# A second pair of heads in seven block products instead of eight, at the start of a fused two-layer block

## The chip, the cores and the metric

The kernel runs on one core of a Trainium2 chip. A core has TensorE (matmuls; PE in the profile), VectorE (DVE), ScalarE (ACT) and GpSimd (POOL), and SyncE (SP), whose queue issues most of the DMAs. The metric is device time in microseconds (us) of one launch, the median over several runs.

## The reference

Eight sequences of 128 tokens by 512 channels go through four residual steps, each of the form x = x + tanh(gate) * f(layernorm(x)): a cross attention with 32 heads and position biases, a dense layer with 4-bit weights, a cross attention with one head, and a dense layer with a router and low-rank experts. The change touches the first attention:

```python
h_q = (x @ w_q.T).reshape(b, lq, H, DH)            # H = 32 heads of DH = 128
h_k = (key_value_states @ w_k.T).reshape(b, lk, H, DH)
score = jnp.einsum('bqhd,bkhd->bhqk', h_q, h_k) + position_bias[None]
```

and the router's map from 15 outputs to 8 experts:

```python
mapped = expert_map[topk_i]
onehot = (mapped[..., None] == jnp.arange(E)).astype(x.dtype)
```

## The kernel before

**Exactness.** Every float32 operand of a large matmul is split into a high part (a rounded copy, made on ScalarE) and a low part (the rest, by a subtraction on VectorE or GpSimd); `split` (L168) does both. A product is then three matmuls, high by high, high by low, low by high (`product`, L172).

**Keys and queries.** Heads are worked in 16 pairs. For one pair and all tokens the product is a 2 by 2 matrix of blocks of weights (two heads by two halves of the 512 channels) times a 2 by 2 matrix of blocks of the context (two halves of the channels by two halves of the tokens: B11, B12, B21, B22). Done plainly that is eight block products; `project_plainly` (L568) makes it with 48 matmuls of 128x512 (lines 591 to 593) and four copies out (L597). `seven` (L214) makes it with seven block products, P1, P5, P6, P2, P7, P4, P3, of six matmuls each (lines 178, 179, 182), which need sums and differences of blocks on both sides:

- of the context, T1 to T4, made once in `context_operands` (L460): differences on VectorE (L488), high parts on ScalarE (L471), low parts one half on GpSimd and one half on VectorE (L474);
- of the weights, for each pair: `pair_sums` (L296) makes three sums on VectorE (L303 to L305), and `pair_parts` (L308) splits the seven parts (L169 and L170) and makes the fourth sum (L315). With `BY_POOL`, the low parts of P1, P2 and P4 are GpSimd's.

The products of `seven` share three PSUM banks: P1, P6, P7 and P4 add up in the same bank c1, and ScalarE copies it out in between (L246, L253, L262, L268); VectorE adds the others (L257, L263, L272).

**The order.** `keys_and_queries` (L953) walks over the pairs. The first two (`PLAIN = 2`) are made plainly, since T1 to T4 are not there yet; in the same stretch the context's differences and pair 2's parts are made. From then on the products of a pair stand among the last ones of the pair before (L974), the parts of the next pair are cast between them, and the normalised rows of x for the queries are made (`query_operands`, L492: statistics, scaling L451 and L454, transposes L505).

TensorE's order is the order written (`in_order`). On the other engines a scheduler sets the order when the program is built; `behind(name)` asks that an instruction be placed behind a marked one on the same engine, and is no wait. Buffers come from rings by tag: the raw weights have 7 buffers (`raw`), so a load can wait for the casts of an earlier pair.

**The experts' map.** `ffn1_weights` (L1383), which belongs to the last layer, loads the map `em_i`, casts it to float (L1397) and compares it with the expert numbers (L1401, L1404). The load and the cast have no inputs from elsewhere, so the scheduler places them early, among the first pairs.

Of the kernel before, what the change touches and what calls it, by code (L numbers as in the profile page):

```python
# [66 lines left out]
def kernel(  # L67
# [37 lines left out]
    nc = tc.nc  # L105
# [9 lines left out]
    def slot(shape, tag, name, dtype=F32):  # L115
        return sb.tile(shape, dtype, tag=tag, name=name, bufs=TAGS[tag])

    def page(shape, name, dtype=F32R):


        return slot(shape, "page", name, dtype)

    def wide_row(tag, name, dtype=F32):
        return slot([P, D], tag, name, dtype)
# [4 lines left out]
    def wide(t):  # L129

        return t.bitcast(F32)


    marks = {}
# [4 lines left out]
    @contextmanager  # L139
    def behind(*names):  # L140
        with ExitStack() as stack:
            for name in names:
                stack.enter_context(tc.issue_after(marks[name]))
            yield
# [23 lines left out]
    def split(high, low, src, low_engine=None):  # L168
        mark("high", nc.scalar.copy(high, src))  # L169
        mark("low", (low_engine or nc.vector).tensor_tensor(low, src, wide(high), ALU.subtract))  # L170
# [105 lines left out]
    def run(steps):  # L276
        for _ in steps:
            pass
# [4 lines left out]
    def load(key, src, shape=(P, D)):  # L283
        t = slot(list(shape), "raw", f"raw_{key}")
        mark("load", nc.sync.dma_start(out=t, in_=src))
        raws[key] = t

    def load_pair(kind, p):
        if p < NP:
            w = {"wk": wk, "wq": wq}[kind]  # L290
            for h in (2 * p, 2 * p + 1):
                load(f"{kind}_{h}", w[:, h])
# [15 lines left out]
    def pair_parts(kind, p, sums, parts, by_pool=()):  # L308

        for which in LEFT:  # L310
            t = parts[which] = slot([P, 2, N], "v", f"{kind}{which}_{p}", F32R)
            with behind("copy"):
                split(t[:, 0], t[:, 1], sums[which], nc.gpsimd if which in by_pool else nc.vector)
            if which == "P2":
                nc.vector.tensor_tensor(sums["P3"], sums["P2"], sums["P6"], ALU.subtract)  # L315
            yield
# [143 lines left out]
    def context_operands():  # L460

        ops = right_pages("cx")
        ops["B12"] = page([P, 2, HK, HALF * P], "cxB12")
        blocks = {
            n: [cx_raw.pop((half, 2 * inner + i)) for i in range(HK)]
            for n, half, inner in (("B11", 0, 0), ("B12", 1, 0), ("B21", 0, 1), ("B22", 1, 1))
        }

        def put(n, i, src, engine=nc.vector):
            o = ops[n]  # L470
            nc.scalar.copy(o[:, 0, i, :], src)  # L471
            mark(
                "low",
                engine.tensor_tensor(o[:, 1, i, :], src, wide(o[:, 0, i, :]), ALU.subtract),  # L474
            )

        for n, pair in blocks.items():
            for i, t in enumerate(pair):
                put(n, i, t)
        marks["lows"] = marks["low"]  # L480
        yield ops
        b11, b12, b21, b22 = blocks.values()
        for n, dst, one, two in (
            ("T1", b11, b12, b11), ("T2", b11, b22, b11), ("T3", b12, b22, b12), ("T4", b21, b21, b11)
        ):
            for i in range(HK):
                with behind("lows"):
                    nc.vector.tensor_tensor(dst[i], one[i], two[i], ALU.subtract)  # L488
                    put(n, i, dst[i], (nc.gpsimd, nc.vector)[i])
        yield ops  # L490
# [424 lines left out]
    BY_POOL = ("P1", "P2", "P4")  # L915
    BEFORE = NP - 2
    order = [("keys", p) for p in range(BEFORE)] + [("queries", p) for p in range(NP)]
    order += [("keys", p) for p in range(BEFORE, NP)]
    def whole_pair(p):

        both, rows = [], []
        for h in range(2 * p, 2 * p + 2):
            both.append([wide_row("v", f"wk_{n}{h}", F32R) for n in "hl"])
            t = raws.pop(f"wk_{h}")
            rows.append(t if p else t.rearrange("p dc n -> p (dc n)"))
        step = D if p else N
        for at in range(0, D, step):
            for (high, low), t in zip(both, rows):
                cols = slice(at, at + step)
                split(high[:, cols], low[:, cols], t[:, cols])  # L930
        return both

    PLAIN = 2

    def later():

        return behind(*(n for n in ("copy", "add") if n in marks))

    left = whole_pair(0)
    making = context_operands()  # L940
# [3 lines left out]
    sums, before = None, iter(())  # L944

    def sums_of(n):
        if n < len(order):
            k, q = order[n]
            return pair_sums("w" + k[0], q)
# [3 lines left out]
    def keys_and_queries():  # L953
        nonlocal left, sums, before
        for n, (kind, p) in enumerate(order[:-1]):
            if n < PLAIN:
                if n + 2 < len(order):
                    load_pair("w" + order[n + 2][0][0], order[n + 2][1])
                if n + 1 == PLAIN:
                    following = {}  # L960
                    run(pair_parts("wk", n + 1, sums_of(n + 1), following))
                    sums = sums_of(n + 2)
                project_plainly(kind, p, left, of_context)
                left = following if n + 1 == PLAIN else whole_pair(p + 1)
                if n == 0:
                    next(making)
                continue
            following = {}
            k, q = order[n + 1]
            casts = pair_parts("w" + k[0], q, sums, following, BY_POOL if n < BEFORE else ())  # L970
            now = project(kind, p, left, of_context if kind == "keys" else rows[-1])
            left = following

            for i, which in enumerate((now, now, before, now, before, now, now)):  # L974
                next(which, None)
                next(casts, None)
                if n == BEFORE // 2 and i == 3:

                    with later():
                        rows.append(next(of_rows))  # L980
                if i == 0:
                    if n + 2 < len(order):
                        load_pair("w" + order[n + 2][0][0], order[n + 2][1])
                    else:
                        load_quad(0)
            before = now
            with behind("add"):
                sums = sums_of(n + 2)
            if n == 3:
                with later():  # L990
                    prep_mask()
            if n < BEFORE:
                with later():
                    rows.append(next(of_rows))
            if 14 <= n < 14 + NB:
                with later():
                    residual(n - 14)
            if n >= BEFORE - 3:
                for _ in range(2 - n % 2):
                    next(extra, None)  # L1000
        parts = quad_parts(0)
        for _ in range(2):
            next(parts)
        for u in range(FIRST):
            fetch(u)
        run(before)
        run(extra)
        run(parts)

    with in_order(*ORD):  # L1010
        keys_and_queries()
# [371 lines left out]
    def ffn1_weights():  # L1383
        for dc in range(NDC):
            t = page([P, 2, 2, NS], f"bw{dc}")
            nc.sync.dma_start(out=wide(t).rearrange("p a h n -> p a (h n)"), in_=bw_kept[:, dc])
            for half in range(2):
                bw[dc, half] = [t[:, part, half] for part in range(2)]
        t = page([P, 2, D], "lora")
        nc.sync.dma_start(out=wide(t), in_=lora_kept)  # L1390
        lora.extend(t[:, part] for part in range(2))
        nc.sync.dma_start(out=rb, in_=router_b.partition_broadcast(P))

        em_i = keep([P, NR], "em_i", I32)
        nc.sync.dma_start(out=em_i, in_=expert_map.partition_broadcast(P))
        em_f = keep([P, NR], "em_f")
        nc.vector.tensor_copy(em_f, em_i)  # L1397
        e_i = slot([P, NE, NR], "moved", "e_i", I32)
        nc.gpsimd.iota(e_i, pattern=[[1, NE], [0, NR]], base=0, channel_multiplier=0)
        nc.vector.tensor_copy(twice, e_i)  # L1400
        nc.vector.tensor_tensor(  # L1401
            twice, twice, em_f.unsqueeze(1).to_broadcast([P, NE, NR]), ALU.is_equal
        )
        nc.vector.tensor_scalar_mul(twice, twice, 2.0)  # L1404
        yield
# [123 lines left out]
```

## Time and profile before

| | us |
|---|---|
| median of 3 runs | 908.09 (907.79 to 909.52) |
| span of the profiled execution | 907.1 |
| TensorE busy | 900.8 (99%) |
| VectorE busy | 673.1 (74%) |
| ScalarE busy | 503.0 (55%) |
| GpSimd busy | 460.3 (51%) |
| first pair's matmuls begin | 5.21 |
| second pair's matmuls, plain | 17.46 to 28.34 |
| third pair's first matmul | 28.34 |

Times in the profile count from the start of the span. A line of a timeline gives the start, the time from first start to last end, the engine, the line of the code, the operation, output and inputs, shapes, and how many instructions were merged; in brackets stands the idle time of that engine before it and what ended it. Matmuls overlap, so their durations are longer than their distance; the distance is read from the starts.

### The profile page before, as it was taken

What the parts mean: (1) busy time and instruction counts of PE and PEld (TensorE: products, weight loads), DVE (VectorE), ACT (ScalarE), POOL (GpSimd) and SP (SyncE); (2) the same over time, 40 slices, a digit from 0 to 9 for tenths busy, and PEclk for the clock granted to TensorE, in tenths of its full rate; (3) what the DMA queues carried; (4) which work ended last, traced back from release to release, by engine and by line L of the source; (5) the groups of instructions that cost most, each with busy time, mean ns of one, the idle gap of its engine ahead of it and who ended that gap; (6) DMA issues with size and microseconds to landing.
All of it is one profiled execution on the core that took longest, in us unless ns stands there. A gap on an engine that the chain in (4) does not pass through costs nothing.

```text
span 907.1 us, 16427 instructions
## 1 busy us (share of the span) xinstructions
PE 900.8 (99%) x5381; PEld 799.2 (88%) x5381; DVE 673.1 (74%) x1353; ACT 503.0 (55%) x1426; POOL 460.3 (51%) x513
## 2 busy tenths in 40 slices
PE   9999999999999999999999999999999999999998
PEld 7888888888888899999999999999999998888897
DVE  7888878789889866777677667666686877565587
ACT  6666555667555545545536445453454544588862
POOL 2355534114322436756747657583866844265441
PEclk9999999999999999999999999999999999999999
DMA  7755477889875956667574765766767566814001
GB/s 256 255 162 163 152 205 232 294 280 285 275 238 204 298 196 186 182 193 221 163 238 151 203 215 153 222 176 201 215 165 208 180 178 177 306 47 143 1 24 71
DMA packets 125223, 174.99 MB, mean 193 GB/s; under 512 B 17105, under 2 KB 54737, under 8 KB 124113
## 3 DMA queue, kind: packets, MB, share of 16 engines
q1 hardware_dynamic: 124992, 173.68, 61.5%
q8 instruction: 42, 0.69, 0.3%
q14 instruction: 45, 0.36, 0.1%
q10 hardware_dynamic: 144, 0.26, 0.1%
HBM read 109.86 MB, written 64.03 MB: 192 GB/s over the span
## 4 chain that ended last, share of the span: by engine, by line
PE 93%; DVE 3%; DMA 2%; ACT 1%; issue 0%; POOL 0%; SPq 0%; DVEq 0%; ACTq 0%; POOLq 0%
PE c_v L178 7%; PE c_v L179 6%; PE c_v L182 6%; PE pso L182 6%; PE pso L178 6%; PE pso L179 6%; PE sc L692 6%; PE av L756 6%; PE c_q L178 6%; PE c_q L179 6%; PE c_q L182 6%; PE c_k L178 4%; PE c_k L179 4%; PE c_k L182 4%; PE tph L1127 1%; DMA cxraw<-in_cxT_dram 1%
## 5 line engine op out<-in xcount | busy, mean ns | idle before, releaser
L709 ACT ACTIVATE s<-s,nm 128x128 f32<-128x128 f32 x256 | 99.8, 392 | 78.8 <-DVE nm L699 54.8
L777 DVE SCALAR_TENSOR_TENSOR x<-pso,tg,x 128x512 f32<-128x512 f32 x128 | 93.4, 741 | 52.2 <-PE pso L182 51.3
L717 POOL TENSOR_TENSOR s<-s,rs 128x512 f32<-128x512 f32 x64 | 66.7, 1042 | 111.1 <-DVE rs L715 63.2
L178 PE MATMUL pso<-wo_h,a 128*128 128x512 f32 x256 | 101.9, 411 | 0.0
L179 PE MATMUL pso<-wo_l,a 128*128 128x512 f32 x256 | 101.5, 397 | 0.0
L182 PE MATMUL pso<-wo_h,a 128*128 128x512 f32 x256 | 101.0, 395 | 0.1
L178 PE MATMUL c_v<-wvP,cxT 128*128 128x256 f32 x288 | 84.8, 294 | 0.2 <-ACT v L253 0.2
L182 PE MATMUL c_v<-wvP,cxT 128*128 128x256 f32 x288 | 81.4, 283 | 0.0
L179 PE MATMUL c_v<-wvP,cxT 128*128 128x256 f32 x288 | 81.4, 283 | 0.0
L757 ACT CAST a<-av 128x512 fp32r<-128x512 f32 x64 | 37.4, 584 | 74.4 <-PE av L756 74.0
L679 POOL TENSOR_TENSOR s<-mneg,bias 128x512 f32<-128x512 bf16 x64 | 75.9, 1186 | 0.1
L756 PE MATMUL av<-pT,v 128*128 128x128 f32 x512 | 71.2, 274 | 0.0
L756 PEld LDWEIGHTS av<-pT,v 128*128 128x128 f32 x512 | 67.1, 191 | 2.8
L692 PE MATMUL sc<-k,q 128*128 128x128 f32 x464 | 65.8, 274 | 0.0
L692 PEld LDWEIGHTS sc<-k,q 128*128 128x128 f32 x464 | 61.9, 191 | 3.2
L178 PE MATMUL c_v<-wvP,cxB 128*128 128x256 f32 x216 | 62.1, 289 | 0.0
L758 DVE TENSOR_TENSOR a<-av,a 128x512 fp32r<-128x512 f32 x64 | 43.4, 679 | 24.9 <-ACT a L757 24.5
L179 PE MATMUL c_v<-wvP,cxB 128*128 128x256 f32 x216 | 61.2, 283 | 0.0
L182 PE MATMUL c_v<-wvP,cxB 128*128 128x256 f32 x216 | 61.1, 283 | 0.0
L170 POOL TENSOR_TENSOR wo_l<-raw_wo,wo_h 128x512 fp32r<-128x512 f32 x32 | 41.4, 1293 | 33.8 <-ACT wo_h L169 33.8
L182 PEld LDWEIGHTS pso<-wo_h,a 128*128 128x128 f32 x256 | 48.2, 188 | 10.8 <-DVE a L758 1.3
L695 DVE TENSOR_TENSOR s<-sc,s 128x512 f32<-128x512 f32 x64 | 43.7, 683 | 17.1 <-PE sc L692 12.4
(277 smaller groups left out, 2808.4 us busy)
## 6 DMA issues: line engine op xcount, KB each, us to landing
keys<-keys SPq DMA_DIRECT2D x64, 256.0 KB, 3.5
queries<-queries SPq DMA_DIRECT2D x64, 256.0 KB, 3.5
through<-s SPq DMA_DIRECT2D x64, 256.0 KB, 2.6
moved<-through SPq DMA_DIRECT2D x256, 64.0 KB, 3.0
q<-queries SPq DMA_DIRECT2D x58, 256.0 KB, 3.8
k<-keys SPq DMA_DIRECT2D x58, 256.0 KB, 4.3
raw_wq<-in_wq_dram SPq DMA_DIRECT2D x32, 256.0 KB, 3.9
raw_wv<-in_wv_dram SPq DMA_DIRECT2D x32, 256.0 KB, 4.9
```

Of the source, the lines that this page charges most:

```text
L170: mark("low", (low_engine or nc.vector).tensor_tensor(low, src, wide(high), ALU.subtract))
L178: nc.tensor.matmul(out, lhsT=lh, rhs=rh, start=first, stop=False, **more)
L179: nc.tensor.matmul(out, lhsT=lh, rhs=rl, start=False, stop=False, **more)
L182: nc.tensor.matmul(out, lhsT=ll, rhs=rh, start=False, stop=last, **more),
L679: nc.gpsimd.tensor_tensor(s, mneg[:, half], bias.unsqueeze(2).to_broadcast([P, NQ, HALF, Q32]), ALU.add)
L692: nc.tensor.matmul(ps[:, j, :], lhsT=q[:, cols], rhs=k[:, cols], start=True, stop=True)
L695: nc.vector.tensor_tensor(s, by_block(ps), s, ALU.add)
L709: e = nc.scalar.activation(one, one, AF.Exp, bias=nm[:, j : j + 1], accum_out=sm[:, j : j + 1])
L717: mark(f"norm{u}", nc.gpsimd.tensor_tensor(s, s, factors, ALU.mult))
L756: nc.tensor.matmul(av[:, b, :], lhsT=v[:, cols], rhs=pT[:, b, :], start=True, stop=True)
L758: mark("al", nc.vector.tensor_tensor(al, av, wide(ah), ALU.subtract))
L777: "x", nc.vector.scalar_tensor_tensor(xs[b], ps, factor, xs[b], ALU.mult, ALU.add, **out)
```

## The change

`PLAIN` becomes 1: only the first pair is made plainly. Behind it the rest of the context's operands (T1 to T4) is made, then the parts of the second pair (called pair 1 in the code, as counting starts at 0), with GpSimd's share as for the later pairs; the second pair goes through `seven`. The load of pair 2's weights stays, and pair 3's loads are issued in the step of the second pair. In `pair_parts` the mark "copy" is used only where it exists. The first rows of x are still made from the same step on (`PLAIN < n`). The cast of the experts' map is placed behind the latest low part of the attention's output ("al"), near the end.

```diff
@@ pair_parts
-            with behind("copy"):
+            with behind(*("copy",) * ("copy" in marks)):
                 split(t[:, 0], t[:, 1], sums[which], nc.gpsimd if which in by_pool else nc.vector)
@@
-    PLAIN = 2
+    PLAIN = 1
@@ keys_and_queries
             if n < PLAIN:
-                if n + 2 < len(order):
-                    load_pair("w" + order[n + 2][0][0], order[n + 2][1])
-                if n + 1 == PLAIN:
-                    following = {}
-                    run(pair_parts("wk", n + 1, sums_of(n + 1), following))
-                    sums = sums_of(n + 2)
+                load_pair("wk", 2)
                 project_plainly(kind, p, left, of_context)
-                left = following if n + 1 == PLAIN else whole_pair(p + 1)
-                if n == 0:
-                    next(making)
+                next(making)
+                left = {}
+                run(pair_parts("wk", 1, sums_of(1), left, BY_POOL))
+                sums = sums_of(2)
                 continue
@@
-            if n < BEFORE:
+            if PLAIN < n < BEFORE:
                 with later():
                     rows.append(next(of_rows))
@@ ffn1_weights
         em_f = keep([P, NR], "em_f")
-        nc.vector.tensor_copy(em_f, em_i)
+        with behind("al"):
+            nc.vector.tensor_copy(em_f, em_i)
```

## Prediction

> **What bounds the kernel now.** I read the page's busy line and the shares of the chain first, then who TensorE waited for, then each engine's timeline around the changed place, 12 to 29 us. The page:
>
> ```profile
> PE 900.8 (99%) x5381; PEld 799.2 (88%) x5381; DVE 673.1 (74%) x1353; ACT 503.0 (55%) x1426; POOL 460.3 (51%) x513
> ...
> PE 93%; DVE 3%; DMA 2%; ACT 1%; issue 0%; POOL 0%; SPq 0%; DVEq 0%; ACTq 0%; POOLq 0%
> ```
>
> All the waits of TensorE in the whole span (longest us last):
>
> ```profile
> PE idle L412 <- POOL ident masks.py:199: 1.4, 1, 1.4
> PE tpx L505 <- DVE xq L454: 0.5, 1, 0.5
> PE c_k L591 <- ACT cxB L471: 0.5, 1, 0.5
> PE c_v L178 <- ACT v L253: 0.2, 1, 0.2
> ```
>
> TensorE is the path. Behind 5.2 us it waits 0.5 + 0.2 us until the last stage, so a matmul removed is time gained, and, just as much, a hole made early is found again at the end: nothing later is there to swallow it. TensorE's timeline, at the start, where the second pair begins, and where it ends:
>
> ```profile
> 5.80 0.63 PE L592 MATMUL c_k<-cxB,wk_l 128*128 128x512 f32 x1
> 6.22 0.63 PE L593 MATMUL c_k<-cxB,wk_h 128*128 128x512 f32 x1
> 6.65 0.52 PE L591 MATMUL c_k<-cxB,wk_h 128*128 128x512 f32 x1
> ...
> 17.46 0.39 PE L591 MATMUL c_k<-cxB,wk_h 128*128 128x512 f32 x1
> ...
> 28.34 0.39 PE L178 MATMUL c_k<-cxB,wkP 128*128 128x512 f32 x1
> ```
>
> From 17.46 to 28.34 stand the 48 matmuls of the second pair in the plain way, 10.88 us or 0.2267 us each, without a hole. In that same time the other engines make the differences of the context (T1 to T4), which the plain way does not need. VectorE, GpSimd and ScalarE:
>
> ```profile
> 14.01 0.68 DVE L170 TENSOR_TENSOR wk_l<-raw_wk,wk_h 128x512 fp32r<-128x512 f32 x1
> 14.62 1.78 DVE L488 TENSOR_TENSOR cxraw<-cxraw,cxraw 128x512 f32<-128x512 f32 x1
> 18.13 2.48 DVE L488 TENSOR_TENSOR cxraw<-cxraw,cxraw 128x512 f32<-128x512 f32 x4
> 20.54 5.19 DVE L474 TENSOR_TENSOR cxT<-cxraw,cxT 128x512 fp32r<-128x512 f32 x3
> ```
> ```profile
> 14.28 1.57 POOL L474 TENSOR_TENSOR cxT<-cxraw,cxT 128x512 fp32r<-128x512 f32 x1 [12.95 <-ACT cxT L471]
> 19.53 5.64 POOL L474 TENSOR_TENSOR cxT<-cxraw,cxT 128x512 fp32r<-128x512 f32 x3 [3.69 <-ACT cxT L471]
> ```
> ```profile
> 18.84 1.67 ACT L471 CAST cxT<-cxraw 128x512 fp32r<-128x512 f32 x3 [3.11 <-DVE cxraw L488]
> 21.88 1.15 ACT L471 CAST cxT<-cxraw 128x512 fp32r<-128x512 f32 x2
> ```
>
> A VectorE subtraction of 128x512 costs 0.62 us alone (2.48 for four). Beside GpSimd's it costs 1.73 (5.19 for three): the two engines take turns, and a turn of both is 0.61 + 1.13. So the differences are ready only at 25.2 (GpSimd) and 25.7 (VectorE). Today nobody waits: TensorE first reads T1 at 29.7.
>
> The Trainium skill has this rule in "SBUF — State Buffer", Who interferes with whom: a VectorE instruction with two SBUF inputs and a GpSimd one that reads SBUF take an exclusive turn at a shared port. The rows agree; without that rule the sum would be the lower end worked out below.
>
> **The change part by part.**
>
> *Removed from TensorE.* 48 plain matmuls become 7 products x 6 = 42 of the same shape: 6 x 0.2267 = 1.36 us gained. The matmuls behind pair 1 keep their order in the built program.
>
> *Removed from the others.* The second pair's two whole casts: ScalarE 2 x 0.62 at 12.18 and 13.05, VectorE 2 x 0.61 (the 14.01 row and one at 16.32). T2's differences wait behind the latter, so they come 1.2 us earlier, and ScalarE's cast of T2 starts at 17.64 in place of 18.84.
>
> *Added.* Pair 1's seven parts of 128x256: seven ScalarE casts (0.31 apart), four sums and four low halves on VectorE (0.335 apart where alone, from 25.65, 25.98, 26.32), three low halves on GpSimd (0.73 alone, some 0.65 in turns). What decides is where they stand. In the changed program's order:
> - ScalarE: the five remaining casts of T2 to T4 and two of pair 0's copies, then the cast of P1. By today's spacing (0.52 a cast, 0.48 a copy): T2, T3, T3, T2, T4 are five casts, then copy, T4, copy. From 17.64 this gives 21.7, the cast ends at 22.1.
> - GpSimd: the lows of T2, T3 and T4, and behind them the low of P1, for which the third matmul of pair 1 waits.
> - VectorE: behind T4's difference (ends 19.4) a sum, T3's low, two sums, T2's low, T4's low, and only then the lows of P5 and P6 and P3's sum.
> - ScalarE again: the copy of the first product (L246) stands behind the cast of P3's part, which waits for that last sum; and the third product (P6) adds into the bank that L246 reads.
>
> *The sum, by turns of the port.* GpSimd's T2 low ends at 20.56 (today 21.76, less 1.2). Then in turns, GpSimd 1.13 or 0.65, VectorE 0.61 or 0.335: sum 20.9, T3 low 22.0, T3's other low 22.6, T4 low 23.7, sum 24.05, P1 low 24.7, sum 25.05, P2 low 25.7, T2 low 26.3, P4 low 27.0, T4 low 27.6, then VectorE alone: P5 low 27.95, P6 low 28.25, sum 28.6. So TensorE:
> 1. First two matmuls of P1 at 22.2 (today 17.46), the third at 24.75, where without a hole it would be at 17.91: 6.84 us lost. P1 ends at 25.66.
> 2. P5: two matmuls, then its low half at 27.95, where it would go on at 26.1: 1.85 us more. P5 ends at 28.85.
> 3. P6: P3's cast ends at 29.05, the copy L246 runs 28.95 to 29.55, P6 at 29.6: 0.75 us more.
> From there P2 covers the copy before P7, and pair 2's parts are ready before pair 1's P7 ends (33.7). Lost: 6.84 + 1.85 + 0.75 = 9.44 us; net of the matmuls 9.44 - 1.36 = 8.1.
>
> *The clock.* No operation of the trace shows a hole of 4.7 us. At the start matmuls came 0.42 apart until 6.65 and 0.23 apart from 7.01, 5.6 us after the first (1.38). From below: the pace stays, 0. From above: the slow pace for 5.6 us from 27.95 is 13 matmuls at 0.19 more, less the 0.75 of step 3 that hides it: 1.8. I take 0.4: counted from 24.75 the 5.6 us end at 30.35, where P5's last four and two of P6 were slow, 6 x 0.19 less what the 0.75 hides; this end is nearer, since TensorE does work between the holes. The Trainium skill, "TensorE: Matmul & The Clock Gate", Part 1, speaks against the change here: about 3.4 us without matmuls halves TensorE's clock until about 3.4 us of work have passed; by that rule alone, counted from 27.95, the term would be an estimated 0.8.
>
> *The map's cast (L1397).* Today it holds VectorE 2.46 us for its DMA, from 31.99 to 34.45, and the only wait of TensorE in reach is the 0.5 at the row statistics' transposes (L505, 45.7). That wait goes, also because TensorE comes there 8 us later: -0.5. In the tail the cast (0.60) stands with the compare and the scaling (0.28 + 0.22, today at 778) just behind VectorE's L758 of 790.8, in front of four additions before each of which VectorE is idle 0.6 us; the first comes 0.5 late, the four gaps take that up, and TensorE shows no wait there: 0, at most 0.5 without that cover.
>
> *Loads.* Pair 3's two loads move behind seven smaller transfers in SP's queue and wait for buffers that pair 1's parts free (the last at 28.6, P3's sum). Landing 4.4 us later, at 33 to 34; TensorE needs them seven products behind 33.7, at 43: 0. The stores of pair 1 move from L598 to L564, four as before; nobody reads them for 100 us.
>
> Sum: 8.1 + 0.4 - 0.5 + 0 = +8.0. The profiled execution's span is 907.1, the median of the runs 908.09, so 1.0 lies around it. Span 915.1, time **916.1 us**.
>
> **Bounds.** From below: VectorE and GpSimd do not hinder each other. Then P1's low ends 0.65 + 0.08 behind its cast, at 22.85, P5 and P6 are in time, 4.94 lost: 4.94 - 1.36 - 0.5 = +3.1, 911.2. From above: GpSimd's three parts at 0.84 (its 30.87 row), +0.6; the clock at 1.8, +1.4; the map's 0.5; and pair 2 meets one more order like step 3 on ScalarE, up to 2: 920.6.
>
> **Rivals.**
> - *Casts are not hindered (or hardly):* ScalarE's queue alone sets the hole. For it: the cast at 22.1 doesn't depend on the port. Against: 5.19 for three. 911.2 to 914.
> - *The slow clock and more:* the half pace lasts, and a later pair starves too. For it: 0.42 us at the start. Against: the work between the holes. 918.6 to 922.
> - *Not slower:* P1's parts are cast in GpSimd's idle stretch, 15.85 to 18.3, before T2's. The loads are there (the cast at 13.05 today shows it); the price is then 908.1 - 1.36 - 0.5 = 906.3. It decides if P1's third matmul starts before 17.91 + 1.83 = 19.7. Against it: the built order has P1's low behind T4's low, whose difference does not even exist before 19.4.
> - *Only the map's cast counts,* the parts being ready: 907.6. The same order speaks against it.
>
> **How the numbers follow.** Forecast (914 to 918.6) 0.71; little hindrance (911.2 to 914) 0.12; more than 918.6 0.14; the two not slower 0.03 together. A range of 912 to 920.5 leaves out about half of the second case, a fifth of the third and the last: 0.12, less than 0.2, because the port's turns are rebuilt by hand. 0.2% (1.8 us) is about what this kernel's runs can tell. Faster 0.02, same 0.01, slower 0.97.
>
> **What would show it.** In the changed profile: TensorE waits of 4 to 5 and about 2 us at pair 1's P1 on ScalarE's cast and GpSimd's L170, one near 2 us at P5 on VectorE's L170, a short one at P6; GpSimd's P1 low near 24.0 to 24.7; pair 2's first matmul near 33.7; the rest shifted whole. The forecast is wrong if P1's third matmul starts before 22 us, if TensorE goes on waiting in pair 2 or 3, or if the shift of about 8 us at 40 us is not there at 800 us.

## The result and the profile after

The changed kernel takes 916.2 us (median of 5 runs, 915.62 to 917.12) against 908.1 before: ratio 1.0087, 95% interval 1.0075 to 1.0100. It is slower by about 8.1 us. The profiled execution, the slowest of the five (917.12 us), has a span of 915.3 us (907.1 before).

The page's busy line: TensorE has six matmuls fewer and is still busy 99% of a span that is 8.2 us longer. Its busy time rose by 1.6 us, because some matmuls ran slowly.

```profile
PE 902.4 (99%) x5375; PEld 799.3 (87%) x5375; DVE 676.2 (74%) x1359; ACT 503.7 (55%) x1431; POOL 464.6 (51%) x519
```

All of TensorE's waits of the changed kernel (us in total, how often, longest), but for those of the start-up and the one of 0.2 us at the values, which both were there before:

```profile
PE c_k L178 <- ACT wkP L169: 6.0, 1, 6.0
...
PE c_k L182 <- POOL wkP L170: 0.8, 1, 0.8
...
PE c_k L182 <- DVE wkP L170: 0.3, 1, 0.3
```

Three waits of the second pair are new: for ScalarE's cast of P1, for GpSimd's low half of P1 and for VectorE's low half of P5. The 0.5 us at the transposes (L505) is gone. Here is TensorE's timeline behind the first pair, whose last matmul started at 16.33:

```profile
22.72 0.79 PE L178 MATMUL c_k<-cxB,wkP 128*128 128x512 f32 x1 [6.00 <-ACT wkP L169]
23.31 0.63 PE L179 MATMUL c_k<-cxB,wkP 128*128 128x512 f32 x1
24.75 0.80 PE L182 MATMUL c_k<-cxB,wkP 128*128 128x512 f32 x1 [0.81 <-POOL wkP L170]
25.34 0.63 PE L178 MATMUL c_k<-cxB,wkP 128*128 128x512 f32 x1
25.77 0.63 PE L179 MATMUL c_k<-cxB,wkP 128*128 128x512 f32 x1
...
27.99 0.79 PE L182 MATMUL c_k<-cxT,wkP 128*128 128x512 f32 x1 [0.32 <-DVE wkP L170]
...
29.44 0.59 PE L182 MATMUL c_k<-cxT,wkP 128*128 128x512 f32 x1
29.86 0.39 PE L178 MATMUL c_k<-cxT,wkP 128*128 128x512 f32 x1
30.09 0.40 PE L179 MATMUL c_k<-cxT,wkP 128*128 128x512 f32 x1
...
33.99 0.39 PE L178 MATMUL c_k<-cxB,wkP 128*128 128x512 f32 x1
```

The 30 matmuls from P1 to P7 would take 6.80 us without a hole. They take 33.99 - 16.56 = 17.43, so 10.63 us are lost: 7.74 up to P1's third matmul (24.75 in place of 17.01), 1.88 from there to P5's third, 0.96 to P6's first. From 22.72 to 29.86 the matmuls come 0.42 to 0.43 us apart where they follow each other (0.59 to 0.60 for the first two behind a wait), afterwards 0.23. The table by stretches (length; busy time of TensorE, weight loads, VectorE, ScalarE, GpSimd; granted TensorE clock; DMA share; GB/s) has that as a clock of 0.71:

```profile
17.40:35.00 17.60, 11.15 (x35) 8.00 (x36) 15.95 (x25) 10.30 (x26) 10.26 (x9) 0.71 0.61 179
```

Asked in smaller stretches, the granted clock is 1.00 up to 19.61, 0.50 from there to 29.85, and 1.00 again behind. So it fell inside the long wait, before P1's first matmul.

Why P1 is late stands in the timelines of VectorE, GpSimd and ScalarE. ScalarE casts P1 (22.26) only behind the casts of T2 to T4, which wait for VectorE's differences until 18.18, and behind two copies. VectorE's first sum and the low half behind it run in turns with GpSimd's lows (22.36: 1.75 us for one subtraction that takes 0.61 alone), and GpSimd's low of P1 stands behind its three lows of T2 to T4:

```profile
17.47 3.56 DVE L488 TENSOR_TENSOR cxraw<-cxraw,cxraw 128x512 f32<-128x512 f32 x4
20.95 1.48 DVE L303 TENSOR_TENSOR more_wk<-raw_wk 128x256 f32<-128x256 f32 x1
22.36 1.75 DVE L474 TENSOR_TENSOR cxT<-cxraw,cxT 128x512 fp32r<-128x512 f32 x1
...
26.99 1.28 DVE L170 TENSOR_TENSOR wkP<-more_wk,wkP 128x256 fp32r<-128x256 f32 x2
28.20 0.41 DVE L315 TENSOR_TENSOR more_wk<-raw_wk,more_wk 128x256 f32<-128x256 f32 x1
```
```profile
18.88 4.68 POOL L474 TENSOR_TENSOR cxT<-cxraw,cxT 128x512 fp32r<-128x512 f32 x3 [2.48 <-ACT cxT L471]
23.52 1.17 POOL L170 TENSOR_TENSOR wkP<-raw_wk,wkP 128x256 fp32r<-128x256 f32 x1
```
```profile
18.18 2.70 ACT L471 CAST cxT<-cxraw 128x512 fp32r<-128x512 f32 x5 [1.91 <-DVE cxraw L488]
...
22.26 0.41 ACT L169 CAST wkP<-raw_wk 128x256 fp32r<-128x256 f32 x1
...
28.64 0.41 ACT L169 CAST wkP<-more_wk 128x256 fp32r<-128x256 f32 x1 [2.31 <-DVE more_wk L315]
28.95 0.58 ACT L246 COPY keys<-c_k 128x512 f32<-128x512 f32 x1
```

What is lost there is never given back. The last transpose of L505 starts 7.8 us later than before (132.8 against 125.0), and so do the first of the attention's output products (358.9 against 350.9, 8.0) and the last (803.6 against 795.4, 8.2).

### The profile page after: what moved, and what is told of

Same layout as the page of the kernel before. It is cut to its first block, busy times and chain, and to the rows that moved or that the text cites. A ratio compares the mean times of both kernels' runs of the same rounds, so it can differ in the third digit from the quotient of the medians.

```text
span 915.3 us, 16446 instructions
## 1 busy us (share of the span) xinstructions
PE 902.4 (99%) x5375; PEld 799.3 (87%) x5375; DVE 676.2 (74%) x1359; ACT 503.7 (55%) x1431; POOL 464.6 (51%) x519
## 4 chain that ended last, share of the span: by engine, by line
PE 95%; DMA 2%; DVE 2%; ACT 1%; SPq 0%; issue 0%; DVEq 0%; ACTq 0%
PE c_v L178 6%; PE c_v L182 6%; PE c_v L179 6%; PE pso L178 6%; PE pso L182 6%; PE pso L179 6%; PE sc L692 6%; PE av L756 6%; PE c_q L178 6%; PE c_q L182 6%; PE c_q L179 6%; PE c_k L182 5%; PE c_k L178 5%; PE c_k L179 5%; PE tph L1123 1%; PE o L178 1%
## 5 line engine op out<-in xcount | busy, mean ns | idle before, releaser
L758 DVE TENSOR_TENSOR a<-av,a 128x512 fp32r<-128x512 f32 x64 | 43.5, 679 | 25.7 <-ACT a L757 25.4
L170 POOL TENSOR_TENSOR wkP<-raw_wk,wkP 128x256 fp32r<-128x256 f32 x39 | 33.5, 872 | 46.9 <-ACT wkP L169 44.2
```

The costliest lines, as they stand in the source:

```text
L758: mark("al", nc.vector.tensor_tensor(al, av, wide(ah), ALU.subtract))
```

## The experiments

The theory: the second pair has no parts when TensorE comes, three waits follow one another, and the length of the hole is set by the order on ScalarE and by the turns of VectorE and GpSimd. The rivals: the slow clock makes most of it; or the turns count for little. "Before" ran beside every experiment and had medians of 907.99 to 908.31.

**Holding TensorE busy.** In the changed kernel, 18 matmuls whose result nobody reads, behind the first pair.

```diff
                 project_plainly(kind, p, left, of_context)
+                busy = ptile([P, HALF * P], "sc", "busy")
+                for _ in range(18):
+                    nc.tensor.matmul(busy, lhsT=left[0][0][:, :P], rhs=of_context["B11"][:, 0, 0, :], start=True, stop=True)
```

> The changed kernel with 18 extra matmuls of 128x512 behind the first pair, into a bank that nobody reads, so that TensorE is busy in about 4.1 of the 4.7 to 6 us of the hole. Theory (the hole is set by the other engines' work, and the slow clock lies almost wholly inside the waits): all matmuls of pair 1 start 0.23 apart, but P5's third still waits for VectorE to about 28.0 and P6 for the copy to about 29.6; P6 starts 0.3 earlier than in the changed kernel (29.86), time 915.9, 0.2 to 0.5 us better. Rival (the slow clock is the cost): 13 matmuls 0.2 us faster, 913.7.

Measured: 916.4 us (915.83 to 917.66), ratio 1.0086 (1.0069 to 1.0103). Filling the first wait gains nothing: the rival's 913.7 lies outside the interval, the theory's 915.9 inside it. That does not show the slow clock to be harmless, since it was moved and not removed: P1 and P5 now ran at 0.23 us a matmul, with waits of 1.2, 1.4 and 1.6 us, and the slow pace came behind them, on P6 and P2, where there is nothing left to hide it:

```profile
21.82 0.50 PE L178 MATMUL c_k<-cxB,wkP 128*128 128x512 f32 x1 [1.19 <-ACT wkP L169]
...
23.91 0.50 PE L182 MATMUL c_k<-cxB,wkP 128*128 128x512 f32 x1 [1.35 <-POOL wkP L170]
...
27.16 0.50 PE L182 MATMUL c_k<-cxT,wkP 128*128 128x512 f32 x1 [1.59 <-DVE wkP L170]
...
28.75 0.60 PE L178 MATMUL c_k<-cxT,wkP 128*128 128x512 f32 x1 [0.40 <-ACT keys L246]
29.14 0.63 PE L179 MATMUL c_k<-cxT,wkP 128*128 128x512 f32 x1
29.57 0.63 PE L182 MATMUL c_k<-cxT,wkP 128*128 128x512 f32 x1
...
32.13 0.53 PE L182 MATMUL c_k<-cxB,wkP 128*128 128x512 f32 x1
32.50 0.40 PE L178 MATMUL c_k<-cxB,wkP 128*128 128x512 f32 x1
```

**The turns at the port.** The lows that were GpSimd's, of T1 to T4 and of pair 1, go to VectorE: in the changed kernel (first run), and the part of T1 to T4 alone in the kernel before (second run).

```diff
-                    put(n, i, dst[i], (nc.gpsimd, nc.vector)[i])
+                    put(n, i, dst[i])
-                run(pair_parts("wk", 1, sums_of(1), left, BY_POOL))
+                run(pair_parts("wk", 1, sums_of(1), left))
```

> The changed kernel with all low parts of T1 to T4 and of pair 1 on VectorE, none on GpSimd. Theory (GpSimd's and VectorE's subtractions take turns, 1.13 us of GpSimd against 0.61 on VectorE): although VectorE gets seven more instructions, its rows fall to 0.61 and 0.335 apart, P1's third matmul starts near 23.5 in place of 24.75, P5 and P6 hardly wait, lost 5.5 to 6 us in place of 9.4: 912.1 (911.3 to 913). Rival (the two engines work side by side, and the place in the queues sets the hole): VectorE has more to do, its last lows come later, 916 to 918.

> The kernel before with T1 to T4's low parts all on VectorE. Theory of the turns: VectorE's eight low parts 0.61 us apart, T4 ready near 23 in place of 25.7 although VectorE does all the work; TensorE does not need them before 29.7, so the time stays 908.1 (907.8 to 908.6). Rival (side by side): T4 ready 2.4 us later, near 28, and the third pair waits: 908.5 to 910.

Measured: 915.08 us (913.56 to 915.58; 1.0071, 1.0056 to 1.0086) and 908.18 us (1.0000, 0.9991 to 1.0009). The turns (the rule of the Trainium skill, "SBUF — State Buffer", Who interferes with whom, that the prediction used) are plain in the second run's VectorE: five lows in 3.09 us, 0.61 apart, where three took 5.19:

```profile
19.87 3.09 DVE L474 TENSOR_TENSOR cxT<-cxraw,cxT 128x512 fp32r<-128x512 f32 x5
```

T1 to T4 were not all ready near 23 for all that: the last of the eight lows starts at 25.01, behind a sum that waited 1.71 us for its load (24.67), so they are complete at 25.7, as before.

In the first run P1's third matmul came at 22.95 and 5.5 us were lost up to it, as expected, and P5 and P6 did not wait. The 3 us that are missing from the expected 912.1 are for the most part the clock: with the later waits gone, nothing hides the slow pace. The ten matmuls from 22.95 to 27.38 took 4.43 us in place of 2.27:

```profile
20.80 0.79 PE L178 MATMUL c_k<-cxB,wkP 128*128 128x512 f32 x1 [3.64 <-ACT wkP L169]
21.39 0.63 PE L179 MATMUL c_k<-cxB,wkP 128*128 128x512 f32 x1
22.95 0.79 PE L182 MATMUL c_k<-cxB,wkP 128*128 128x512 f32 x1 [0.94 <-DVE wkP L170]
...
26.95 0.63 PE L182 MATMUL c_k<-cxT,wkP 128*128 128x512 f32 x1
27.38 0.46 PE L178 MATMUL c_k<-cxT,wkP 128*128 128x512 f32 x1
```

**Parts earlier.** The parts of the second pair are written ahead of the first pair's products; P1's cast and low move to the front, the rest stays behind the context's differences.

```diff
+                following = {}
+                run(pair_parts("wk", 1, sums_of(1), following, BY_POOL))
                 project_plainly(kind, p, left, of_context)
                 next(making)
-                left = {}
-                run(pair_parts("wk", 1, sums_of(1), left, BY_POOL))
+                left = following
```

> The changed kernel with pair 1's parts written ahead of the first pair's products, so that the scheduler may take them before T1 to T4; in the built order only P1's cast and low part move ahead (first on ScalarE and GpSimd behind the context's own casts), the rest stays. Theory (three waits in a row, P1, P5, P6, each of its own length): the wait at P1 goes, and the one at P5 grows to 7.0 us, until its low part behind T2's, T3's and T4's at about 26.3; P6 in time; 913.7 (913 to 915). Rival (what counts is P1's place in the queues): the hole goes, 906.7 to 908.

Measured: 917.03 us (915.78 to 918.56; 1.0096, 1.0081 to 1.0111). P1 runs straight behind the first pair, and the hole opens one product later, as the theory has it; but it is no cheaper:

```profile
22.77 0.80 PE L178 MATMUL c_k<-cxT,wkP 128*128 128x512 f32 x1 [4.23 <-ACT wkP L169]
23.36 0.63 PE L179 MATMUL c_k<-cxT,wkP 128*128 128x512 f32 x1
26.75 0.80 PE L182 MATMUL c_k<-cxT,wkP 128*128 128x512 f32 x1 [2.76 <-DVE wkP L170]
27.34 0.63 PE L178 MATMUL c_k<-cxT,wkP 128*128 128x512 f32 x1
...
30.75 0.46 PE L182 MATMUL c_k<-cxT,wkP 128*128 128x512 f32 x1
31.06 0.40 PE L178 MATMUL c_k<-cxB,wkP 128*128 128x512 f32 x1
```

Is it the clock that the expectation missed here? The same kernel, with TensorE kept busy through both waits (matmuls whose result nobody reads, 18 ahead of P5 and 11 between its second and third):

```diff
+        if name == "k1":
+            dummies(18)
         c3 = ptile(shape, "av", f"c3_{name}")
@@ product
             nc.tensor.matmul(out, lhsT=lh, rhs=rl, start=False, stop=False, **more)
+            if i == 0 and between:
+                dummies(between)
```

> The kernel with the second pair's parts traced early (e5_early, 917.03 us), with matmuls whose result nobody reads in TensorE's two waits: 18 of 128x512 ahead of P5, and 11 between P5's second and third. Theory (e5_early missed its 913.7 because the slow pace of 0.42 us a matmul comes out behind the waits): with TensorE busy through both waits the slow pace does not come, about 2 us are saved: 915.0 us. Rival (the slow pace comes in any case some us later, as in e3_busy): 917.0 us, with a stretch of 0.42 us a matmul behind 27 us.

Measured: 915.14 us (914.86 to 915.26; 1.0076, 1.0062 to 1.0090).

```profile
26.87 0.50 PE L184 MATMUL c_k<-cxT,wkP 128*128 128x512 f32 x1 [0.76 <-DVE wkP L170]
27.20 0.40 PE L178 MATMUL c_k<-cxT,wkP 128*128 128x512 f32 x1
27.44 0.39 PE L179 MATMUL c_k<-cxT,wkP 128*128 128x512 f32 x1
...
29.27 0.39 PE L178 MATMUL c_k<-cxB,wkP 128*128 128x512 f32 x1
```

P5's third matmul starts 0.12 us later than without the extra matmuls, P2's first 1.79 earlier (29.27 against 31.06). So the slow pace cost 1.9 us there, and it does not come when TensorE is kept busy through all the waits. In the first experiment only one wait was filled.

**The order written out.** All lows on VectorE, and the differences, casts and lows of T1 to T4 and of the second pair written in the order in which TensorE needs them: T1, P1, P5, T2, P6, P2 and so on. The second run is the same order with GpSimd's share as in the changed kernel.

```diff
+                with in_order(mybir.EngineType.DVE, mybir.EngineType.Activation, mybir.EngineType.Pool):
+                    next(making)
+                    parts = pair_parts("wk", 1, sums_of(1), following)
+                    next(parts)
+                    next(making)
+                    next(parts)
...
                 project_plainly(kind, p, left, of_context)
+                left = following
```

> The changed kernel with all low parts on VectorE as in e4_vector, and the order of VectorE and ScalarE written out in the order of need: T1, P1, P5, T2, P6, P2, T3, P7, T4, P4, P3, then pair 2's sums; the copies of pair 0's last two banks behind P2's cast, the first sum of pair 1 behind P7's low. Theory (work of 13.5 us from 12.8 on, each piece a little ahead of its product): no wait at P1, P5, P6, P2 and P7; pair 2's first part is cast late (25.7 where TensorE comes at 24.3), 1.5 to 2.5 us lost there: 908.7 (907.3 to 910). Rival (there is too much work for the stretch in any order, so that a hole of 5 us or more stays somewhere): 912 or more.

> The written order of e7_written, but with GpSimd's share of the low parts as in the changed kernel (half of T1 to T4, and P1, P2 and P4). Theory (turns at a shared port: 4 x 1.13 + 3 x 0.65 of GpSimd in place of 7 cheaper ones of VectorE, 3 us more in the same stretch): a wait of about 1 us at P6 and more at P7 and P4, 2 to 4 us slower than e7_written: 911.5 (910 to 913). Rival (side by side): VectorE is relieved, 1 to 3 us faster than e7_written.

Measured: 914.19 us (913.8 to 914.49; 1.0064, 1.0049 to 1.0079) and 915.23 us (914.83 to 915.65; 1.0078, 1.0064 to 1.0092). The first time lies in the rival's range, but not for the rival's reason (too much work in any order): P1 and P5 run without a hole, and at P6 TensorE waits 3.4 us for something that neither had named. ScalarE shows what for (L418 is the tanh of the gates in this kernel, whose lines behind L246 are shifted by one to three):

```profile
19.82 0.20 ACT L418 ACTIVATE tg<-gates_in 128x4 f32<-128x4 f32 x1 [3.81 <-DMA gates_in<-in_g_ffn_dram]
19.94 1.12 ACT L473 CAST cxT<-cxraw 128x512 fp32r<-128x512 f32 x2
```
```profile
23.18 0.50 PE L178 MATMUL c_k<-cxT,wkP 128*128 128x512 f32 x1 [3.41 <-ACT keys L247]
```

A small instruction that waits for its load stood in front of T2's casts, and T2's casts in front of the copy of P1's bank. With GpSimd's share the median is 1.0 us higher, not the 2 to 4 that I expected, and the two intervals overlap. In both runs P6 starts at 23.2 behind the same wait (3.41 and 3.59 us), which hides what the turns cost before it.

**Without the tanh.** The tanh moved behind the cast of P3:

```diff
-    nc.scalar.activation(tg, gates_in, AF.Tanh)
@@ keys_and_queries
                 left = following
+                with behind("high"):
+                    nc.scalar.activation(tg, gates_in, AF.Tanh)
```

> The kernel with the order written out (e7_written), with one thing moved: the tanh of the gates stands behind the cast of P3 on ScalarE, so that the casts of T2 no longer stand behind the gates' load. Theory (a chain that moves its hole): TensorE's wait of 3.4 us at P6 shrinks to about 1.4, which is set by the copy of P1's bank behind the casts of T2, P6 and P2 and two copies of the first pair (21.05 instead of 23.18). VectorE is 2.3 us earlier from T2's differences on, but the third pair of heads comes no earlier than its load and ScalarE's row of casts: its P1 waits about 0.9 and 1.0 and its P5 about 1.8. Lost in all about 5.1 us against 4.8 of waits and 1.6 of slow pace in e7_written: about 912.3 us. If the tanh was the whole cause and nothing else comes late: about 909. If the wait at P6 has another cause: 914.2, as in e7_written.

Measured: 911.42 us (911.12 to 911.92; 1.0036, 1.0023 to 1.0050), 2.8 us less than with the tanh in front. P6 starts at 21.34 (21.05 forecast) with no more than 0.2 us lost, where I had expected a wait of 1.4. Part of that is chance: in this execution the first pair ended at 18.45, against 16.89 with the tanh in front, so TensorE came to P6 1.6 us later. What comes late next is the third pair's P1, as expected, by 1.06 and 0.99 us:

```profile
26.79 0.50 PE L178 MATMUL c_k<-cxB,wkP 128*128 128x512 f32 x1 [1.06 <-ACT wkP L169]
27.13 0.40 PE L179 MATMUL c_k<-cxB,wkP 128*128 128x512 f32 x1
28.52 0.50 PE L182 MATMUL c_k<-cxB,wkP 128*128 128x512 f32 x1 [0.99 <-POOL wkP L170]
```

None of these waits is followed by the slow pace.

**The best order found.** On top of that: P2, which needs no difference, is made ahead of P6; the copy of P1's bank stands ahead of the first pair's copies; the third pair's P1 is cast ahead of T4; P4 and P3 of the second pair are made ahead of the third pair's P5.

```diff
+        for part in (second, sixth) if name == "k1" else (sixth, second):
+            yield from part()
@@ keys_and_queries
+                    copy_out(2)
+                    next(making)
+                    ahead = {"P1": slot([P, 2, N], "v", "wkP1_2", F32R)}
+                    split(ahead["P1"][:, 0], ahead["P1"][:, 1], raws["wk_4"][:, :N])
@@
+            if n == PLAIN + 1:
+                steps = (now, before, before, now, now, now, now)
```

> The best order that I can write down for the changed kernel: tanh later, all lows on VectorE, P2 (which needs no difference) made ahead of P6, the copy of P1's bank ahead of the first pair's copies, the third pair's P1 cast and its low ahead of T4's casts, P4 and P3 of the second pair ahead of the third pair's P5. Theory: TensorE loses about 0.5 us at P7 (lows of T3 ready near 23.3, TensorE there at 22.3), 0.8 at the third pair's P1 (its load lands near 24.7) and 0.5 at P4; no hole is long enough to slow the clock. 1.8 lost against 1.36 saved: 908.5 to 909.0 us, 7 us below the changed kernel and about the time before. If the slow pace follows these short waits too: about 910.5. If the losses of the changed kernel are not a matter of order: above 913.

Measured: 910.68 us (median of 11 runs, 909.74 to 911.43; 1.0028, 1.0019 to 1.0037). Three short waits are left, 2.4 us in all (2.9 us by the starts of the matmuls); the first is for the copy of P6's bank, which I had put behind two copies of the first pair and the third pair's cast:

```profile
PE c_k L178 <- ACT keys L256: 1.3, 1, 1.3
...
PE c_k L178 <- ACT keys L270: 0.6, 1, 0.6
PE c_k L182 <- DVE wkP L170: 0.5, 1, 0.5
```

So order and the engine of the lows account for 5.5 of the 8.1 us. No version that I ran comes below the kernel before; the six matmuls saved (1.36 us) are less than the waits that remain.

**The map's cast.** The changed kernel with the cast back at its old place, and the kernel before with the cast late:

```diff
-        with behind("al"):
-            nc.vector.tensor_copy(em_f, em_i)
+        nc.vector.tensor_copy(em_f, em_i)
```

> The changed kernel with the experts' map cast where it was (no mark on it). Theory (TensorE has no wait left that the cast could shorten, since the hole delays it by 8 us): 916.2, within 0.5 us of the changed kernel. Rival (the cast's 2.46 us on VectorE fall into the hole and lengthen it): up to 918.6.

> The kernel before with only the experts' map cast late. Theory: VectorE's wait of 2.46 us at 32 goes, and with it TensorE's 0.5 us at the transposes of the first rows: 907.6 (907.4 to 908.3); at the end nothing is lost. Rival (the cast among the last additions delays TensorE there): 908.4 to 908.8.

Measured: 915.81 us (915.72 to 916.1; 1.0085, 1.0071 to 1.0099) and 908.27 us (median of 11, 907.58 to 909.77; 1.0002, 0.9993 to 1.0011). In the second, TensorE's wait of 0.5 us at L505 is gone and the time did not move; a gain of 0.5 us is within the interval, so it is neither shown nor excluded. In the first that wait is gone too, with the cast at its old place: in the changed kernel the hole alone takes it away. The cast is no part of the 8 us.

## Why the prediction was right, and where by luck

**The time and the mechanism held.** 916.1 forecast, 916.2 measured. P1's third matmul was put at 24.75 and started at 24.75, with GpSimd's low ending at 24.69 against 24.7 forecast. The cast of P1 ended at 22.67 (22.1 forecast). P5's third matmul started at 27.99 (27.95), and the third pair's first at 33.99 (33.7). The span is another matter: the time lies 1.8 us above the profiled span in every run (917.12 and 915.3 here), not 1.0, so the profiled execution before must have been one of about 908.9 us. Only differences enter the sum, so nothing follows from it.

**Where the closeness is luck.** GpSimd's four lows ended within 0.15 us of the forecast (20.48, 22.15, 23.56 and 24.69). VectorE was a turn late at first (the first sum ended at 22.43 where 20.9 was forecast, the low behind it at 24.11 where 22.6 was) and had caught up at P5's low (27.94, forecast 27.95). And the whole chain moves from execution to execution. In the kernel with the map's cast early and in the one with extra matmuls, whose order here is the same, T2's first cast starts at 17.32 and 17.28 (18.18 here, 17.64 forecast) and P1's third matmul at 23.90 and 23.91. So the turns give the length of the chain; the agreement at 24.75 to a hundredth is chance.

**Removed matmuls.** Six fewer, as counted; the 1.36 us was not measured by itself.

**First wait.** 7.74 us were lost where 6.84 were forecast. The hole ended when it should, but it began 0.9 us earlier, since the first pair ended at 16.56 in this execution (17.46 before), in part because TensorE's clock was granted in full from 5.96 on and not from 6.92. TensorE gained nothing by being early: the end of the hole is set by VectorE, GpSimd and ScalarE. In the sum the two cancel.

**Second and third wait.** 1.88 and 0.96 us against 1.85 and 0.75. But the trace does not show a wait near 2 us at P5, as I said it would: it shows 0.32, and none at P6. The slow matmuls filled the time up to the moment at which the data came. The amounts were right and the sign by which to know them was wrong.

**The clock.** 0.4 forecast. P6 starts at 29.86 where the copy alone would have let it start at 29.53 to 29.6, so the clock added about 0.3. That is right only for this order of work, and even there it depends on the execution: in the kernel with the map's cast early the clock was at half only from 23.36 to 26.77, and P6 started at 28.76, with the copy. Where the later waits were shortened the same slow pace came out at 1.9 to 2.2 us, which is most of why two of my expectations (parts earlier, lows on VectorE) were too low, and part of it for the two written orders. The Trainium skill, "TensorE: Matmul & The Clock Gate", Part 1, has the clock halve after an idle window of some 3.4 us until some 3.4 us of work are done. The runs agree where a long wait is followed by work without a hole: 23.20 to 26.68 with the order written out and GpSimd's share kept, 3.5 us. They do not agree on the idle window: with one wait filled, the clock fell behind a stretch of 3.41 us in which TensorE was busy for 1.46 us, and the measurement decides (the last section has the figures). My own row, the 5.6 us at the kernel's start, was the poorer guide: over the profiles of this case the clock first rises between 4.30 and 9.76 us, while the first matmul starts at 1.38 or 1.39.

**The map's cast.** -0.5 forecast. In the trace it is there: TensorE's lag behind the kernel before falls from 8.37 to 7.86 us at the first transposes. The medians cannot tell it, and the hole alone does it, as the kernel with the cast early shows. **Loads.** Nothing: TensorE has no wait on a load in pairs 2 and 3. **The rest.** The lag of 8.37 us is the 10.63 lost, less 0.90 for the earlier end of the first pair and 1.36 for the six matmuls. Behind the first transposes the shift is 7.8 us up to the last transposes and 8.2 at the end of the attention; these 0.4 us stand under no wait of TensorE, and I leave them open.

**The rivals.** "Casts hardly hindered" fell by the 1.75 us row and by P1 at 24.75. "Slow clock and more" fell by the pairs behind, which do not wait, and by the clock, which is full again at 29.85. "Not slower" needed P1's third matmul before 19.7. When P1 was in fact brought forward, the time was 917.03, since the hole only moves to P5: that rival would not have held even on its own condition.

## What to carry to other kernels

A cheaper algorithm for TensorE is worth its matmuls only if its operands are there when TensorE is; count what the other engines must have finished by then, in the built order, before counting matmuls. When a hole is traced to one late operand, look for the second and the third behind it: moving P1 forward gave nothing, and the 5.5 us came only from several changes of order and of engine together; the largest single one was a tanh of 0.2 us that waited for its load in front of the casts (2.8 us). And where the slow clock overlaps with waits, price a shortened wait with the slow pace added back, since it then comes out on the path.

## What the runs showed of the hardware that I had not expected

- The slow pace (0.42 to 0.43 us a 128x512 matmul in place of 0.23) came also with no wait over 1.6 us: with one wait filled by extra matmuls there were waits of 1.2, 1.4, 1.6 and 0.4 us between about 21 and 28.75, and the eight matmuls behind them were slow. Three waits of 1.06, 0.99 and 0.65 us between 25.3 and 33.6 left the pace at 0.23.
- The clock went by a fixed grid. In each of the 13 profiles of this case, the granted clock is 1.00 or 0.50, and it changes only at whole multiples of 3.41 us from its first rise. Besides the start and the last few microseconds it was at half for 10.24 us in the changed kernel and with the parts earlier, 6.83 with the lows on VectorE, and 3.41 with one wait filled, with the map's cast early and in the two written orders.
- It went by how long TensorE was busy (by the profile) in one stretch of that grid, and not by the longest wait. Over all the stretches of the 13 profiles, without an exception:

| the clock behind the stretch | TensorE busy in the 3.41 us | stretches |
|---|---|---|
| fell from 1.00 to 0.50 | 0.00 to 1.59 us | 14 |
| stayed at 1.00 | 1.95 us or more | 3412 |
| stayed at 0.50 | 0.31 to 2.61 us | 5 |
| rose from 0.50 to 1.00 | 2.87 us or more | 20 |

- So a wait inside the slow stretch can make it longer. In the changed kernel the stretches from 19.61, 23.03 and 26.44 held 0.31, 2.6 and 3.1 us of work, and only the third raised the clock. It need not: with the map's cast early a stretch with waits held 2.87 us and raised it. Why the limits lie where they do, no run here shows.
- Filling one wait of the changed kernel with extra matmuls only put the slow stretch off (916.4 against 916.2 us); with the parts earlier, filling both waits was worth 1.9 us.
